# One more accumulating transfer per half block of layer 3, and wider spacing of the projection and feature pieces, in a fused four-layer attention kernel

## The chip, the cores and the metric

The kernel runs on one core of one Trainium2 chip. The metric is the device time of one execution in microseconds (us); smaller is better. Names of engines: PE is the matrix engine (PEld its weight loads), DVE the vector engine, ACT the scalar engine, POOL the GpSimd engine, SP the engine that only issues transfers (DMAs). L1698 is line 1698 of the kernel before.

## The reference, cut to what matters

The input x has four images of 64 x 64 positions with 64 channels, in float32. Four layers follow one another:

```python
# layer 0: attention over positions (n = 4096 per image)
q, k, v = x@Wq + bq, x@Wk + bk, x@Wv + bv
attn = softmax(q @ k.T)                      # 4096 x 4096 per image
x = gamma * einsum('bmn,bmc->bnc', attn, v) + x
# layer 1: layer norm, pointwise, 3x3 depthwise, gating, pointwise; twice a residual
# layer 2: attention of the rows of the image with themselves, no weights
xf = x.reshape(B, 64, 4096)                  # N = 64*64 columns per "channel"
x = einsum('bcj,bij->bci', xf, softmax(einsum('bci,bcj->bij', xf, xf))) + x
# layer 3: attention with 32 inner channels, then a normalization over all images
f = softmax(theta_x @ phi_x.T)               # 4096 x 4096 per image
w_y = (f @ g_x) @ w_W + w_b
x = x + gamma * (w_y - mean) * rsqrt(var + 0.001) + beta
```

The softmax of layer 3 needs, for every query, the sum of 4096 exponentials. How those sums are formed is what the first part of the change touches.

## The kernel before, in words

The work is one long list of items, run by `run()`: each item issues one score (or four) and what belongs to it; a schedule written by hand says which other pieces go between. The order on PE, ACT, DVE and POOL is exactly the order in which the program issues; each of these engines works its own list from the front. The stages, by the trace: layer 0 of images 0 to 3 (0 to 1026 us, with layer 1 of the earlier images laid between), layer 2 of image 0 (to 1230), layer 2 of image 1 (to 1453), layer 3 of image 0 (to 1597), layer 2 of image 2 (to 1786), layer 3 of image 1 (to 1929), layer 2 of image 3 (to 2119), layer 3 of images 2 and 3 (to 2410), and the end (to 2443). So a layer 3 block is followed by a layer 2 block, save that image 2's is followed by image 3's.

**Two lanes** carry the pieces that go between the items. A `Lane` has a clock; `misc.tick(1.8)` moves it by 1.8 at each score of layer 0 and at each item of image 0's layer 2. A piece runs when the clock has reached the lane's `next`; then `next` grows by what the piece yields. So a yield of 3.4 against ticks of 1.8 puts the pieces after ticks 1, 2, 4 and 6 of a lane that starts empty.

**The projection** `project0(b)` (L1031 on) makes q and v of image b while layer 0 of image b - 1 runs. For b > 0 it has four pieces, in the order once, v, once, v. A "once" piece has 8 matmul passes (L1037), an ACT copy out of PSUM (L1049) and a DVE copy (L1047); a "v" piece has 16 passes (L1064) and two DVE adds (L1066). Layer 0 has only two score slots in PSUM (`take_slots(0, 1)`), used in turn by scores and pieces alike: a piece takes the slot that the score after next would use.

**The features** `features2(b)` (L1303 on) transpose an image for layer 2, in four pieces: four transposes (L1310), one DVE copy and one ACT copy (L1313), two DMAs issued by SP (L1314). For image 0 they run in the lane during layer 0 of image 3, for image 1 during layer 2 of image 0 from its item 89 on (three slots there), for images 2 and 3 at fixed items of a layer 3 block, where the yielded number is not used.

**Layer 3** `layer3(b)` (from L1621) has 64 items per image: two halves (`nb`) of 32 key tiles (`mc` = 0 to 31). An item's `scores` makes 128 x 2048 scores on PE (L1646) and their exponentials e on ACT (L1657, in two or three instructions). Two items later its `products` multiplies e with the values (L1707). The e tiles come from a ring of six (`ep`, `bufs=6`), so item n + 6 writes the tile of item n. For the softmax sums, 23 of the tiles of a half are added on DVE, one after the other, into `esum` (L1696 and L1698; the first add takes tiles 0 and 1). The tiles whose `mc` is in `BY_DMA` (eight of 32) are summed instead by transfers that add to their destination: POOL issues two for each, one per half of the columns, into the tile `st["dma"]` (L1677 the first pair, which only copies, L1679 the others). One more DVE add (L1700) puts that tile into `esum`, after the products of item `by_dma[-1] + 4`. The tile comes from the pool `xn` of one buffer, which layer 2 of images 2 and 3 uses for `xr`, loaded by SP (L1368). Four items after the last tile of a half, `totals` lets PE sum `esum` over the partitions (L1719); the division and the output projection follow (L1742, L1727 to L1737, L1756). The first half of image 2 uses another list, `MORE_BY_DMA`. In the second half of image 3 tiles 30 and 31 are summed by PE (L1691), not by DVE.

Of the kernel before, what the change touches and what calls it, by code (L numbers as in the profile page):

```python
# [691 lines left out]
def fast_path(ctx: ExitStack, tc: tile.TileContext, a: dict, out: bass.AP, bad):  # L692
# [33 lines left out]
    def new_ps():  # L726
        if turn_of["banks"]:
            if turn_of["bank"] % turn_of["banks"] == turn_of["banks"] - 1:
                turn_of["bank"] += 1
            k = new_bank(), new_bank()  # L730
            return PS[:, 512 * k[0] : 512 * k[0] + 1024]
        s = turn_of["slots"][turn_of["ps"] % len(turn_of["slots"])]
        turn_of["ps"] += 1
        return PS[:, bass.ts(s, 1024)]

    def piece():
        if turn_of["banks"]:
            return PS[:, bass.ts(new_bank(), 512)]
        return new_ps()[:, 0:512]
# [8 lines left out]
    def new_e(name="e"):  # L748
        return ep.tile([128, 2048], F32, tag="e", name=name)
# [4 lines left out]
    def new_big(name):  # L754
        return big.tile([128, 4096], F32, tag="big", name=name)
# [228 lines left out]
    def tok(x, s, j):  # L984
        return x[64 * s : 64 * s + 64, bass.ts(j, 512)]
# [6 lines left out]
    def at(i, fn):  # L992
        due.setdefault(i, []).append(fn)
# [33 lines left out]
    def project0(b):  # L1027
        x, m = X[:, b], im[b]
        m.q = new_big("q")
        m.v = new_big("v")[:, 0:2048].rearrange("p (t c) -> p t c", c=C)  # L1030
        once = ((0, "once"), (0, "v"), (1, "once"), (1, "v"))  # L1031
        for j, w in once if b else ((0, "q"), (0, "v"), (1, "q"), (2, "q"), (1, "v"), (3, "q")):
            ps = new_ps()
            if w == "once":
                for o in range(2):
                    for s in range(2):
                        mm(  # L1037
                            ps[64 * o : 64 * o + 64, bass.ts(s, 512)], wq[64 * s : 64 * s + 64, 0:64],
                            tok(x, s, 2 * j + o), start=True, stop=True,
                        )  # L1040
                qs = m.q.rearrange("p (s n) -> p s n", s=2)
                for o in range(2):
                    own, other = slice(64 * o, 64 * o + 64), slice(64 - 64 * o, 128 - 64 * o)
                    n = bass.ts(2 * j + o, 512)
                    src = ps[own, :].rearrange("p (s n) -> p s n", s=2)
                    if o:
                        nc.vector.tensor_scalar_add(qs[own, :, n], src, bqk[own, :])  # L1047
                    else:
                        act(qs[own, :, n], src, AF.Identity, bias=bqk[own, :])  # L1049
                    nc.sync.dma_start(out=qs[other, :, n], in_=qs[own, :, n])  # L1050
            elif w == "q":
                for o in range(0, 128, 64):
                    for s in range(2):
                        mm(
                            ps[o : o + 64, bass.ts(s, 512)], wq[64 * s : 64 * s + 64, o : o + 64],
                            tok(x, s, j), start=True, stop=True,
                        )
                for s in range(2):
                    nc.vector.tensor_scalar_add(
                        m.q[:, 2048 * s + 512 * j : 2048 * s + 512 * j + 512], ps[:, bass.ts(s, 512)], bqk  # L1060
                    )
            else:
                for i in range(8):
                    mm(ps[:, bass.ts(i, 128)], x[:, bass.ts(8 * j + i, 128)], wv, start=True, stop=True)  # L1064
                for s in range(2):
                    nc.vector.tensor_add(  # L1066
                        m.v[:, 16 * s + 8 * j : 16 * s + 8 * j + 8, :],
                        ps.rearrange("p (t s c) -> p t s c", s=2, c=C)[:, :, s, :],
                        bv.unsqueeze(1).to_broadcast([128, 8, C]),
                    )  # L1070
            yield 3.4

# [228 lines left out]
    def features2(b):  # L1303
        x = X[:, b]
        im[b].ko = ko = new_big("ko")
        kv = ko[:, 0:N].rearrange("p (a e n) -> p a e n", e=2, n=128)
        for g in range(4):
            ps = piece()
            for i in range(4):
                nc.tensor.transpose(ps[:, bass.ts(i, 128)], x[:, bass.ts(4 * g + i, 128)], ident)  # L1310
            for e, copy in enumerate((nc.vector.tensor_copy, nc.scalar.copy)):
                own, other = slice(64 * e, 64 * e + 64), slice(64 - 64 * e, 128 - 64 * e)
                copy(kv[own, bass.ts(g, 4), e, :], ps[own, :].rearrange("p (a n) -> p a n", n=128))  # L1313
                nc.sync.dma_start(out=kv[other, bass.ts(g, 4), e, :], in_=kv[own, bass.ts(g, 4), e, :])  # L1314
            yield 3.0

    SIDES = [[(7, (h + 1) % 7), ((h + 2) % 7, (h + 3) % 7)] for h in range(7)]
    FULL = [(7, [7])] + [(h, [h] + SIDES[h]) for h in range(6)] + [(6, SIDES[6] + [6])]
# [217 lines left out]
    def close2(b):  # L1536
        x, m = X[:, b], im[b]
        ps, tot, n = piece(), sums2[:, b, :], 4 * max(m.mirrored) + 4
        cs = m.cs.rearrange("p (j k) -> p j k", k=4)
        for k in range(4):  # L1540
            mm(ps[32 * k : 32 * k + 32, 0:n], sel4, cs[:, 0:n, k], start=True, stop=True)
        g = 0
        while g < 8:
            k = g
            while k < 8 and m.count[k] == m.count[g]:
                k += 1
            nc.vector.tensor_reduce(
                tot[:, 4 * g : 4 * k],
                m.zs[:, m.first[g] : m.first[g] + 4 * m.count[g] * (k - g)]
                .rearrange("p (t k) -> p t k", k=m.count[g]), AX.X, ALU.add,  # L1550
            )
            g = k
        nc.vector.tensor_add(tot[:, 0:n], ps[:, 0:n], tot[:, 0:n])
        rz = sm.tile([128, 32], F32, tag="rz2", name="rz2")
        nc.vector.reciprocal(rz, tot)
        yield
        for i in range(4):
            ps = new_ps()
            for j in range(8):
                c = 1024 * i + 128 * j  # L1560
                nc.tensor.transpose(ps[:, bass.ts(j, 128)], m.A[:, c : c + 128], ident)
            blocks_ = ps.rearrange("p (j n) -> p j n", n=128)
            nc.vector.tensor_mul(
                blocks_, blocks_, rz[:, bass.ts(i, 8)].unsqueeze(2).to_broadcast([128, 8, 128])
            )
            xs = x[:, bass.ts(i, 512)].rearrange("p (j h) -> p j h", h=H)
            for o in range(2):
                nc.vector.tensor_add(xs, ps.rearrange("p (j o h) -> p j o h", j=8, o=2)[:, :, o, :], xs)
            yield
# [1 line left out]


    wys, early = {}, []
    BY_DMA = (2, 5, 8, 11, 14, 17, 20, 23)
    MORE_BY_DMA = (2, 4, 7, 9, 12, 14, 17, 19, 22, 24)
    small, between3 = {}, {}
    held = []
# [40 lines left out]
    def keys3(b):  # L1618
        m = im[b]
        m.ph = new_big("ph")  # L1620
        keys = m.ph.rearrange("p (s n) -> p s n", s=2)  # L1621
        for j in range(4):
            for k in range(4):
                nc.sync.dma_start(
                    out=keys[32 * k : 32 * k + 32, :, bass.ts(j, 512)],
                    in_=m.own[32 * j : 32 * j + 32, :, :],
                )

    def layer3(b):
# [3 lines left out]
        def scores(n):  # L1633
            nb, mc = n // 32, n % 32
            by_dma = MORE_BY_DMA if b == B - 2 and nb == 0 else BY_DMA
            e = es[n] = new_e()
# [46 lines left out]
        def products(n):  # L1683
            nb, mc = n // 32, n % 32
            by_dma = MORE_BY_DMA if b == B - 2 and nb == 0 else BY_DMA
            e, esum = es[n], m.tg[:, 2048:4096]
# [126 lines left out]
    conv_from, misc_from, misc_to = {}, {}, {}  # L1813
# [9 lines left out]
    for b in range(B):  # L1823
        misc_to[len(items)] = True
        f = len(items)
        if b == 0:
            layer2(b)
            misc_from[f + 89] = [features2(b + 1)]
        else:
            layer2(b, lambda b=b: keys3(b - 1))  # L1830
            turns = close2(b - 1)
            for i in (9 if b == 1 else 8, 11, 21, 31, 41):
                at(f + i, lambda turns=turns: next(turns))
            misc_from[f + 46] = [open3(b - 1)]
            f = len(items)
            misc_to[f] = True
            layer3(b - 1)
            if b + 1 < B:
                turns = features2(b + 1)
                for i in (4, 7, 10, 13):  # L1840
                    between3[f + i] = 2, lambda turns=turns: next(turns)
    f = len(items)
# [220 lines left out]
```

## Time and profile before

| what | value |
|---|---|
| median of three runs | 2442.99 us (2442.64 to 2450.58) |
| the profiled execution: its own time | 2444.88 us |
| its span in the trace | 2443.1 us |
| granted TensorE clock | 0.999 |
| busy: PE, ACT, DVE, POOL | 99%, 67%, 60%, 22% |
| layer 3 blocks together (four) | 578 us of the span (144, 143, 145, 146) |
| DVE and ACT busy in one of them (1453 to 1597) | 118.44 and 133.46 of 144 us |
| DMA engines busy in the same stage | 0.63 |

How to read it: the time is measured by the device around the whole execution, the span from the first to the last record of the trace; 1.8 us lie outside the span. Engine times are sums of instruction durations. Those of PE are modelled at their ends, and its instructions overlap, so that PE at 99% can still be waiting; what PE loses shows in the distance from one group of matmuls to the next.

### The profile page before, as it was taken

How to read it: one execution, taken by the hardware profiler on the slowest of the kernel's cores; microseconds unless marked ns; L12 is line 12 of the kernel's file. 1: busy time of each engine (PE TensorE's matmuls, PEld its weight loads, DVE VectorE, ACT ScalarE, POOL GpSimd, SP SyncE). 2: the span in 40 equal slices, each digit the busy share in tenths (PEclk: the TensorE clock that was granted, in tenths of full speed). 3: DMA queues.
4: the chain of work that ended last, by engine and by line, in shares of the span. 5: the costliest groups of instructions: out<-in, count | busy, mean ns of one | idle time of the engine just before them, and what ended most of it. 6: DMA issues, size and time to landing. Idle time of an engine off the chain costs nothing.

```text
span 2443.1 us, 63650 instructions
## 1 busy us (share of the span) xinstructions
PE 2410.9 (99%) x27509; PEld 914.5 (37%) x27509; DVE 1477.5 (60%) x1794; ACT 1642.9 (67%) x3140; POOL 541.1 (22%) x381
## 2 busy tenths in 40 slices
PE   9999999999999999999999999999999999999998
PEld 3343453336333543343344442144421344421113
DVE  2020278227732774278657668876668866688886
ACT  4656766666666666668655459954479744569996
POOL 2000000000000000030136561256631365622110
PEclk9999999999999999999999999999999999999999
DMA  3000000000000000030540027610075300386554
GB/s 80 1 18 1 19 1 18 18 19 1 19 18 5 15 19 18 21 76 2 118 92 19 20 64 138 139 28 23 16 152 118 79 22 21 76 169 141 118 116 117
DMA packets 66373, 131.68 MB, mean 54 GB/s; under 512 B 12860, under 2 KB 34085, under 8 KB 66085
## 3 DMA queue, kind: packets, MB, share of 16 engines
q0 software_dynamic: 23024, 81.83, 16.6%
q1 hardware_dynamic: 42309, 43.85, 7.9%
q8 instruction: 218, 3.57, 0.6%
q10 hardware_dynamic: 752, 1.85, 0.2%
q14 instruction: 70, 0.57, 0.1%
HBM read 4.80 MB, written 4.19 MB: 4 GB/s over the span
## 4 chain that ended last, share of the span: by engine, by line
PE 87%; DVE 5%; ACT 4%; DMA 1%; issue 1%; SPq 1%; POOL 0%; ACTq 0%; DVEq 0%; POOLq 0%
PE PS L1096 18%; PE PS L1122 18%; PE PS L1391 10%; PE PS L1453 10%; PE PS L1646 8%; PE PS L1707 8%; PE PS L1479 7%; PE PS L1206 2%; DVE tg L1698 2%; ACT e L1657 2%; DMA xn<-e 1%; ACT e L1396 1%; PE PS L1064 1%; PE PS L1171 1%; PE PS L1270 1%
## 5 line engine op out<-in xcount | busy, mean ns | idle before, releaser
L1101 ACT ACTIVATE e<-PS 128x1024 f32<-128x1024 f32 x512 | 523.7, 1023 | 339.8 <-PE PS L1096 306.5
L1396 ACT ACTIVATE e<-PS 128x512 f32<-128x512 f32 x632 | 370.9, 595 | 330.2 <-PE PS L1391 312.5
L1096 PE MATMUL PS<-X,q 64*64 64x512 f32 x4096 | 574.0, 591 | 2.3 <-DVE X L979 1.7
L1122 PE MATMUL PS<-e,vq 64*64 64x512 f32 x4096 | 575.3, 592 | 0.0
L1657 ACT ACTIVATE e<-PS 128x512 f32<-128x512 f32 (+2 forms) x588 | 500.1, 920 | 60.3 <-PE PS L1646 38.0
L1698 DVE TENSOR_TENSOR tg<-tg,e 128x2048 f32<-128x2048 f32 x172 | 393.9, 2290 | 42.7 <-ACT e L1657 31.3
L1391 PE MATMUL PS<-ko 64*64 64x512 f32 x2528 | 335.6, 596 | 1.7 <-ACT ko L1313 0.8
L1453 PE MATMUL PS<-e,X 64*64 64x512 f32 x2528 | 329.6, 590 | 1.1 <-ACT own L1465 1.1
L1432 POOL TENSOR_TENSOR esum<-esum,e 128x1024 f32<-128x1024 f32 x132 | 314.1, 2380 | 60.0 <-ACT e L1396 52.7
L1241 DVE SCALAR_TENSOR_TENSOR y<-pad,vec,y 128x1024 f32<-128x1024 f32 x240 | 308.9, 1287 | 18.2 <-ACT y L1237 10.9
L1432 POOL TENSOR_TENSOR esum<-e 128x1024 f32<-128x1024 f32 x22 | 52.2, 2373 | 1192.5 <-ACT e L1396 1184.7
L1409 DVE STREAM_TRANSPOSE turned<-e 128x1024 f32<-128x1024 f32 x196 | 240.6, 1238 | 107.5 <-ACT e L1396 107.2
L1646 PE MATMUL PS<-tg,ph 32*64 32x512 f32 x4096 | 295.7, 612 | 2.5 <-ACT e L1657 1.6
L1096 PEld LDWEIGHTS PS<-X,q 64*64 64x64 f32 x4096 | 183.0, 133 | 261.6 <-issue 181.5
L1122 PEld LDWEIGHTS PS<-e,vq 64*64 64x64 f32 x4096 | 183.1, 133 | 253.7 <-issue 158.5
L1707 PE MATMUL PS<-e,tg 128*32 128x512 f32 x2048 | 272.5, 604 | 0.0
L1109 DVE TENSOR_REDUCE sums<-zs 128x1 f32<-128x4 f32 x128 | 19.7, 154 | 276.0 <-ACT e L1101 275.9
L1679 POOL DMA_DIRECT2D xn<-e x116 | 101.0, 892 | 293.9 <-ACT e L1657 203.1
L1453 PEld LDWEIGHTS PS<-e,X 64*64 64x64 f32 x2528 | 98.0, 133 | 174.7 <-issue 155.1
L1391 PEld LDWEIGHTS PS<-ko 64*64 64x64 f32 x2528 | 90.3, 132 | 169.1 <-issue 145.1
L1646 PEld LDWEIGHTS PS<-tg,ph 32*64 32x64 f32 x4096 | 63.3, 129 | 224.4 <-ACT e L1657 192.0
L1396 ACT ACTIVATION_READ_ACCUMULATOR e<-PS 128x1 f32 x632 | 127.1, 201 | 0.0
(219 smaller groups left out, 1682.2 us busy)
## 6 DMA issues: line engine op xcount, KB each, us to landing
xn<-e POOLq DMA_DIRECT2D x132, 512.0 KB, 5.2
esum<-e POOLq DMA_DIRECT2D x20, 512.0 KB, 5.8
xn<-t SPq DMA_DIRECT2D x64, 128.0 KB
ph<-tg SPq DMA_DIRECT2D x64, 128.0 KB
xn<-X SPq DMA_DIRECT2D x224, 32.0 KB
xr<-X SPq DMA_DIRECT2D x176, 32.0 KB
ko<-ko SPq DMA_DIRECT2D x32, 128.0 KB
xr<-in_x_dram SPq DMA_DIRECT2D x13, 256.0 KB
```

The lines of the kernel that those rows point to most:

```text
L1096: mm(ps[64 * c : 64 * c + 64, bass.ts(r, 512)], m.q[rows_, 128 * t + 64 * c : 128 * t + 64 * c + 64], x[rows_, bass.ts(g, 512)], start=Tru ...
L1101: act(es[g // 2][:, bass.ts(g % 2, 1024)], ps, AF.Exp, bias=SHIFT0, accum_out=zs[:, g : g + 1],)
L1122: ins = mm(PS[64 * s : 64 * s + 64, 2048 + 512 * j : 2560 + 512 * j], vq[rows_, :], es[j // 2][rows_, k : k + 512], start=t == 0 and i < 2 ...
L1241: stt(y1, win, wt, y1, ALU.mult, ALU.add)
L1391: mm(ps[64 * c : 64 * c + 64, bass.ts(r, 512)], m.ko[rows_, k : k + 64], m.ko[rows_, bass.ts(h, 512)], start=True, stop=True,)
L1396: act(e[:, bass.ts(r, 512)], ps[:, bass.ts(r, 512)], AF.Exp, bias=SHIFT2, accum_out=slot(g, 2 * u + r),)
L1432: nc.gpsimd.tensor_add(esum, st["e"][mine_t[h][0]] if k == 1 else esum, e)
L1453: mm(st["acc"][r][64 * c : 64 * c + 64, :], xw[rows_, 4 * g + 2 * u + c, :], st["e"][n][rows_, bass.ts(c, 512)], start=n == mine[h][0], st ...
L1646: mm(PS[64 * c : 64 * c + 64, bass.ts(banks[k], 512)], m.ph[32 * k : 32 * k + 32, 128 * mc + 64 * c : 128 * mc + 64 * c + 64], m.th[32 * k ...
L1657: act(e[:, 512 * lo : 512 * k], PS[:, 512 * banks[lo] : 512 * banks[lo] + 512 * (k - lo)], AF.Exp,)
L1698: nc.vector.tensor_add(esum, esum, e)
L1707: mm(st["y"][32 * k : 32 * k + 32, :], m.gx[:, i % 32, :], es[i][:, bass.ts(k, 512)], start=mc == 0, stop=i % 32 == 31,)
```

## The change

```diff
@@ project0
-            yield 3.4
+            yield 3.7 if b else 3.4
@@ features2
-            yield 3.0
+            yield 3.7
@@ layer 3
-    BY_DMA = (2, 5, 8, 11, 14, 17, 20, 23)
+    BY_DMA = (2, 5, 8, 11, 14, 17, 20, 23, 26)
     MORE_BY_DMA = (2, 4, 7, 9, 12, 14, 17, 19, 22, 24)
@@ the schedule, at layer 2 of image 0
         if b == 0:
             layer2(b)
-            misc_from[f + 89] = [features2(b + 1)]
+            misc_from[f + 88] = [features2(b + 1)]
```

In seven of the eight half blocks of layer 3, tile 26 is summed by two more accumulating transfers in place of a DVE add, and the add of the transfers' tile into `esum` moves from after the products of item 27 to after those of item 30. The first half of image 2 keeps its list. The projection's pieces for images 1 to 3 and the features' pieces in the lane yield 3.7. Features of image 1 start one item earlier. Nothing else changes: the same matmuls, exponentials and copies are issued.

## The prediction, made before the changed kernel was run

> **What bounds the kernel now.** I read the page first, then the waits, then the timeline around each place that the diff touches. The page says that PE is always busy, and that ACT and DVE are not:
>
> ```profile
> PE 2410.9 (99%) x27509; PEld 914.5 (37%) x27509; DVE 1477.5 (60%) x1794; ACT 1642.9 (67%) x3140; POOL 541.1 (22%) x381
> L1698 DVE TENSOR_TENSOR tg<-tg,e 128x2048 f32<-128x2048 f32 x172 | 393.9, 2290 | 42.7 <-ACT e L1657 31.3
> ```
>
> The 99% is soft. Inside layer 0 a score group (8 passes) starts 1.72 us after the one before it, product included; that is PE's own pace. In layer 3 an item has 16 score passes, eight side by side, and 8 product passes, four side by side: again four rounds, 1.72 us at layer 0's 0.43 a round. Yet items start 2.04 us apart, which is ACT's pace (1.94 us of exponentials and a gap of about 0.1). So a microsecond taken from DVE counts only where something waits for DVE. The group of the sums over partitions names that place:
>
> ```profile
> L1719 PE MATMUL PS<-tg,ones 128*32 128x512 f32 x64 | 8.5, 601 | 2.6 <-DVE tg L1698 2.6
> ```
>
> PE idles 2.6 us in all before these sums because DVE has not finished adding. The first such place, at the middle of image 0's block (DVE first, then PE and ACT):
>
> ```profile
> 1508.00 9.48 DVE L1698 TENSOR_TENSOR tg<-tg,e 128x2048 f32<-128x2048 f32 x4 [1.37 <-ACT e L1657]
> 1517.52 2.29 DVE L1700 TENSOR_TENSOR tg<-tg,xn 128x2048 f32<-128x2048 f32 x1
> 1519.91 9.48 DVE L1698 TENSOR_TENSOR tg<-tg,e 128x2048 f32<-128x2048 f32 x4
> ...
> 1527.42 1.57 PE L1646 MATMUL PS<-tg,ph 32*64 32x512 f32 x16
> 1529.54 1.06 PE L1719 MATMUL PS<-tg,ones 128*32 128x512 f32 x8 [0.55 <-DVE tg L1698]
> 1532.53 1.95 ACT L1657 ACTIVATE e<-PS 128x512 f32<-128x512 f32 x2 [1.44 <-PE PS L1646]
> ```
>
> DVE adds tiles 24 to 27, the transfers' tile, then 28 to 31: nine adds, one every 2.39 us, without a gap; items come every 2.04 us, so the backlog grows to the end. PE stands 0.55 us, and ACT then 1.44 us. The other three places show 0.55 (1862.36), 0.61 (2277.21) and this:
>
> ```profile
> 2345.86 1.06 PE L1719 MATMUL PS<-tg,ones 128*32 128x512 f32 x8 [0.84 <-DVE tg L1698]
> ```
>
> At the blocks' ends before a layer 2 (1599.36 and its twin) and in the tail (2409.95) PE is itself late, and no such idle is shown.
>
> For the spacing, compare image 1's projection, where "once" and "v" are already two scores apart, with image 2's, where the first two pieces are one score apart:
>
> ```profile
> 154.68 1.04 PE L1096 MATMUL PS<-X,q 64*64 64x512 f32 x8
> 155.54 1.04 PE L1122 MATMUL PS<-e,vq 64*64 64x512 f32 x8
> 156.70 1.09 PE L1096 MATMUL PS<-X,q 64*64 64x512 f32 x8
> 157.72 2.05 PE L1064 MATMUL PS<-wv,X 128*128 128x128 f32 x16
> ```
>
> ```profile
> 375.62 1.30 PE L1096 MATMUL PS<-X,q 64*64 64x512 f32 x8
> 376.54 1.29 DVE L1047 TENSOR_SCALAR q<-PS,bqk 64x1024 f32<-64x1024 f32 x1 [2.36 <-ACT q L1049]
> 377.89 2.05 PE L1064 MATMUL PS<-wv,X 128*128 128x128 f32 x16 [0.97 <-DVE q L1047]
> ```
>
> The "v" piece takes the slot that "once" used, and DVE empties that at 377.83 only. Two scores later it would have been free.
>
> **What the Trainium skill says.** "Perfetto Trace Analysis", section "Tensor Engine Instruction (MATMUL, LD_WEIGHTS)": PE's end times are computed, not observed, while ACT and DVE are strict queues. The trace agrees: PE at 99% has starts 0.3 us late, as above, and I therefore price by starts. "SBUF — State Buffer", section "SBUF: two separate sides": compute and DMA can't slow each other there, and a DVE operation with two SBUF inputs loses only to a GpSimd operation that reads SBUF. The trace agrees: the adds take 2.29 us whether transfers run or not. "DMA: Bandwidth & Descriptors", section "Issuing engines are not separate DMA queues": all transfers share 16 engines. In the trace a pair of accumulates fills them: busy share 1.0 at about 200 GB/s for about 5.3 us of every 6.1 (three items).
>
> **The change, part by part.**
>
> Layer 3, DVE. In seven half blocks one add of 2.39 us goes. The tail of a half becomes 24, 25, 27, 28, 29, 30, transfers' tile, 31. Image 0: exp(24) ends at 1507.96 and exp(27) three items later, at 1514.1; DVE has finished 25 at 1512.7 and waits 1.4 us. From 1514.1 six adds of 2.39 end at 1528.4, against 1529.40 now. So 2.39 - 1.4 = 1.0 us is gained on DVE, and the sums could start at 1528.5; but the scores before them end at 1528.99 by the record. PE is next late, and the gain is the idle shown, 0.55 us. Same working: image 1 61.2 against 62.2, gain 0.55; end of image 2, 76.1 against 77.1, gain 0.61; middle of image 3, 44.3 against 45.7, gain 0.84. Sum 2.55 us. From below, 0, if PE's record hides another wait; from above, the whole excess of the distance over 2.04 + 0.86 (an item and the sums): 3.97 - 2.90 = 1.07 three times and 1.51 once, 4.7 us. I take 2.55: ACT idles 1.4 to 1.8 us behind each place, so that PE's gain is passed on.
>
> The other three halves gain nothing. At the ends of images 0 and 1 DVE finishes at 1597.0 in place of 1597.97, and PE reaches the sums at 1599.36 either way. In the tail PE is in L1691 until 2410.1 and DVE has ended at 2409.56; then 2408.6.
>
> Layer 3, transfers: two more of 512 KB per half, each 0.87 us of POOL's issue. POOL has nothing after them until the next half's first pair (1529.50) or layer 2's sums (1604.67), so the issue costs 0. The pair of tile 23 leaves the DMA engines at 1512.9, 1846.5, 2261.0 and 2329.0 in the middle halves, and 2398.2 in the tail; another 5.3 us brings tile 26 to 1518.2, 1851.8, 2266.3, 2334.3 and 2403.5. Two things wait for it. Tile 32's exponential reuses the e tile, at 1522.35, 1855.2, 2269.95, 2338.3: cover 3.4 to 4.2 us. The add of the transfers' tile, now about 2406.3 in the tail: cover 2.8 us. Behind the waiting DVE add stands only tile 31's add, then PE's sums. Cost 0 while the cover holds.
>
> The moved add frees `xn` later: at 1525.9 for 1519.8 in the middle, where the next half's first transfer starts at 1529.50 (cover 3.6), and at 1594.6 for 1588.4 before layer 2, where SP's loads wait for it. The 16 loads of `xr` land at 1598.1 now, 1604.3 then; PE needs them at 1612.69 (L1479). Cover 8.4 us, cost 0; the next 16 loads follow on SP's queue for a use some 25 us later.
>
> Projection. Image 2: from the score at 375.62 to that at 394.56 are seven intervals of 1.72, a "once" of 0.86 and two "v" of 1.98, which is 16.86; it took 18.94, so 2.08 is lost. Image 1, already spaced, from 152.10 to 174.26: 21.16 of work, 22.16 taken, 1.0 lost. The lane's sums put the pieces after ticks 1, 3, 5, 7 instead of 1, 2, 4, 6; image 2 becomes like image 1: 1.0 us gained, and image 3 (18.95 for the same stretch) likewise. Image 1's own second piece goes from two to three scores after the first: 0. Together 2.0, between 1.0 (if the conv work on DVE makes the copy late) and 2.4.
>
> Features of image 0: each piece costs 0.17 us in a stretch of 18.46, none waits for another; spacing changes nothing. Features of image 1: pieces after items 88, 90, 92, 94 instead of 89, 90, 92, 94. The second piece now comes one item after the first, and the score behind it waits:
>
> ```profile
> 1219.90 1.09 PE L1391 MATMUL PS<-ko 64*64 64x512 f32 x8 [0.82 <-ACT ko L1313]
> ```
>
> One item earlier the first ACT copy ends at about 1217.7 instead of 1219.85; exp(89) then stands behind it (1219.2 for 1217.5) but exp(90) ends at 1220.6 for 1221.2, and the second piece's copy at 1223.15 for 1223.6. Gain 0.45, between 0 and 0.8. Its DMAs on SP shift with it, ahead of nothing.
>
> **Sum**: 2.55 + 2.0 + 0.45 = 5.0 us off the profiled execution, 2444.88 to 2439.9, with the span from 2443.1 to 2438.1. That execution stood 1.9 us over the median of the runs shown; off the median, 2442.99 - 5.0 = **2438.0 us**, or 0.2% less. About 0.3% (7.3 us) is what a measurement of this kernel can tell from no change, so the likeliest case counts as no change.
>
> **Rivals.**
> *More than the idle shows.* PE's modelled ends hide part of the wait: 4.7 in layer 3, 2.4 + 0.8 elsewhere, and up to 0.8 for what follows the sums: 8.7 us, 2434.3. For it: ACT's idle exceeds PE's. Against: the score group at 1527.42 is stretched to 1.57 by held exponentials, not by DVE.
> *Only the spacing shows.* Layer 3 runs at ACT's pace and takes the DVE time back: 2.45 us off, 2440.5. Against it stand the four named idles.
> *Slower: the ninth pair holds its tile.* If tile 26 lands more than about 9 us after tile 23's pair (5.3 reckoned), exp(32) waits, and from 8.1 us the tail's add. The longest landing of one such transfer is 9.7 us. At 12 us the four middles lose 2.5 + 3.3 + 3.1 + 2.7, the tail 2.4 (3.9 late, less the 1.5 by which DVE would lead PE), 14.0 in all, and 2.45 of the gain is left: 11.5 slower, 2454.5. Against: spacing stays at three items, as for the eight before, and nothing else moves then.
>
> **Chances.** Forecast 0.58, more 0.22, only spacing 0.12, slower 0.08. Forecast and spacing lie within 0.3%: 0.70; the larger gain lies beyond it: 0.22; the slower case 0.08. Range: from 2433.5 (just under all upper bounds) to 2444.0 (all gains zero, and 1 us for moved pieces), leaving out the slower case and a little on both sides.
>
> **What would show it.** 172 adds at L1698 become 165 and L1679 has 130 issues for 116. The idle before L1719 falls from 2.6 us to near 0, and DVE waits about 1.4 us before tile 27. The stretches of images 2 and 3 take about 17.9 us. Wrong would be: an exponential or L1700 waiting for a transfer, L1479 waiting for `xr`, or layer 3's middles unchanged with the idle before L1719 gone.

## The result and the profile after

The changed kernel takes **2439.2 us** (2438.12 to 2440.64, 16 runs) beside 2445.05 (2442.48 to 2450.58, 16 runs) for the kernel before on the same chips: a ratio of 0.9975, with a 95% interval of 0.9968 to 0.9982. By that ratio it is 6.1 us less (4.4 to 7.8), by the medians 5.9. The executions of the kernel before reach further up (a quarter of them above 2446.9 us) than those of the changed kernel, and the lower quartiles, 2442.90 and 2438.75, are only 4.2 us apart. The forecast was 2438.0 us, as 5.0 us less than 2442.99. Its base turned out low: over more runs the kernel before has a median of 2444 to 2445.6.

The profiled execution of the changed kernel has its own time of 2438.81 us, a span of 2437.0 and a granted clock of 0.999. The engines and three groups, from the page and the list of groups (columns as before: busy us and mean ns, then the idle time ahead and what ended it):

```profile
PE 2408.3 (99%) x27509; PEld 914.1 (38%) x27509; DVE 1461.6 (60%) x1787; ACT 1643.0 (67%) x3140; POOL 553.5 (23%) x395
L1698 DVE TENSOR_TENSOR tg<-tg,e 128x2048 f32<-128x2048 f32 x165 | 377.8, 2290 | 51.1 <-ACT e L1657 40.9
L1679 POOL DMA_DIRECT2D xn<-e x130 | 113.3, 898 | 319.5 <-ACT e L1657 225.9
L1719 PE MATMUL PS<-tg,ones 128*32 128x512 f32 x64 | 8.5, 602 | 2.2 <-DVE tg L1698 1.1 <-ACT e L1657 1.1
```

165 adds and 130 issues: the change does what it says. But the idle ahead of the sums over partitions (L1719) is 2.2 us, not near 0. Of it 1.1 stand in one place, the middle of image 2's block, whose list the change leaves alone; there it comes and goes (none when the changed kernel ran again). The other 1.1 are new: four times 0.26, in the four places of the forecast, and ended by **ACT**. The timeline of the changed kernel at the middle of image 0's block (start, busy us, engine and line; lines of other work left out):

```profile
1509.91 9.49 DVE L1698 TENSOR_TENSOR tg<-tg,e 128x2048 f32<-128x2048 f32 x4 [1.43 <-ACT e L1657]
1519.43 2.29 DVE L1700 TENSOR_TENSOR tg<-tg,xn 128x2048 f32<-128x2048 f32 x1
...
1521.22 0.58 ACT L1713 COPY yz<-PS 128x512 f32<-128x512 f32 x1 [0.44 <-PE PS L1707]
1521.70 5.19 ACT L1657 ACTIVATE e<-PS 128x1536 f32<-128x1536 f32 x6
1521.83 2.29 DVE L1698 TENSOR_TENSOR tg<-tg,e 128x2048 f32<-128x2048 f32 x1
...
1523.21 1.57 PE L1646 MATMUL PS<-tg,ph 32*64 32x512 f32 x16
...
1525.04 1.06 PE L1719 MATMUL PS<-tg,ones 128*32 128x512 f32 x8 [0.26 <-ACT e L1657]
...
1528.04 1.94 ACT L1657 ACTIVATE e<-PS 128x512 f32<-128x512 f32 x2 [1.15 <-PE PS L1646]
```

DVE waits 1.43 us ahead of tile 27 and then runs tiles 27 to 30, the transfers' tile and tile 31 without a gap, as forecast. It ends at 1524.12, 0.9 us before the sums start. ACT is what is late now: it copies the finished products (L1713), then runs exponentials without a pause.

**Where the time went, by a ladder.** Both kernels run the same 1732 exponentials in the same order. I took the start of each in one trace less its start in the other; where that lag steps and stays, time is won.

| place | forecast | ladder |
|---|---|---|
| first loads (second exponential) | 0 | 0.68 |
| projection, images 1, 2, 3 | 0, 1.0, 1.0 | 0, 0.77, 0.79 |
| features of image 1 | 0.45 | 1.11 |
| layer 2 of image 0, 1237 to 1247 us | 0 | 0.86 |
| layer 3 middles and end: 1529, 1862, 2277, 2346 us | 0.55, 0.55, 0.61, 0.84 | 0.29, 0.29, 0.35, 0.58 |
| middle of image 2, unchanged list | 0 | 0.37 |
| sum | 5.0 | 6.1 |

So three rows of the forecast are there, each with another size, and three rows are not in it. The experiments had to say which rows belong to the change. The first score groups of image 2's projection and of image 1's features in the changed kernel, for the two spacings:

```profile
374.94 1.30 PE L1096 MATMUL PS<-X,q 64*64 64x512 f32 x8
375.80 1.30 PE L1122 MATMUL PS<-e,vq 64*64 64x512 f32 x8
377.21 1.09 PE L1096 MATMUL PS<-X,q 64*64 64x512 f32 x8
378.23 2.05 PE L1064 MATMUL PS<-wv,X 128*128 128x128 f32 x16
```

```profile
1214.76 0.58 ACT L1313 COPY ko<-PS 64x512 f32<-64x512 f32 x1 [0.77 <-DVE ko L1313]
...
1215.39 0.65 PE L1310 MATMUL PS<-ident,X 128*128 128x128 f32 x4 [0.17 <-ACT ko L1313]
...
1216.89 1.04 PE L1391 MATMUL PS<-ko 64*64 64x512 f32 x8
...
1219.66 0.58 ACT L1313 COPY ko<-PS 64x512 f32<-64x512 f32 x1 [1.88 <-DVE ko L1313]
```

The "v" piece (L1064) no longer waits 0.97 us for the copy on DVE, and the score at L1391 no longer waits 0.82 us for the copy on ACT.

### The profile page after: what moved, and what is told of

Read it like the earlier page. It is cut to its first block, busy times and chain, and to the rows that moved or that the text cites. A ratio compares the mean times of both kernels' runs of the same rounds, so it can differ in the third digit from the quotient of the medians.

```text
span 2437.0 us, 63657 instructions
## 1 busy us (share of the span) xinstructions
PE 2408.3 (99%) x27509; PEld 914.1 (38%) x27509; DVE 1461.6 (60%) x1787; ACT 1643.0 (67%) x3140; POOL 553.5 (23%) x395
## 4 chain that ended last, share of the span: by engine, by line
PE 90%; DVE 4%; ACT 4%; issue 1%; DMA 0%; SPq 0%; ACTq 0%; DVEq 0%
PE PS L1096 18%; PE PS L1122 18%; PE PS L1391 10%; PE PS L1453 10%; PE PS L1646 9%; PE PS L1707 9%; PE PS L1479 7%; PE PS L1206 2%; ACT e L1657 2%; DVE tg L1698 1%; ACT e L1396 1%; PE PS L1171 1%; PE PS L1270 1%; PE PS L1561 1%; PE PS L1064 1%
## 5 line engine op out<-in xcount | busy, mean ns | idle before, releaser
L1698 DVE TENSOR_TENSOR tg<-tg,e 128x2048 f32<-128x2048 f32 x165 | 377.8, 2290 | 51.1 <-ACT e L1657 40.9
L1391 PE MATMUL PS<-ko 64*64 64x512 f32 x2528 | 334.3, 596 | 0.9 <-DVE X L1568 0.5
L1679 POOL DMA_DIRECT2D xn<-e x130 | 113.3, 898 | 319.5 <-ACT e L1657 225.9
L1391 PEld LDWEIGHTS PS<-ko 64*64 64x64 f32 x2528 | 90.0, 132 | 167.8 <-issue 145.5
```

The costliest lines, as they stand in the source:

```text
L1391: mm(ps[64 * c : 64 * c + 64, bass.ts(r, 512)], m.ko[rows_, k : k + 64], m.ko[rows_, bass.ts(h, 512)], start=True, stop=True,)
L1698: nc.vector.tensor_add(esum, esum, e)
```

## The experiments

In each run the kernel before ran on the same chip. The us are the ratio's interval on a time before of 2444.

| kernel | median us | before | ratio (95%) | us against before |
|---|---|---|---|---|
| spacing only | 2441.03 | 2444.3 | 0.9984 (0.9976 to 0.9991) | -5.9 to -2.2 |
| projection only | 2442.43 | 2445.15 | 0.9991 (0.9984 to 0.9998) | -3.9 to -0.5 |
| features only | 2442.91 | 2444.1 | 0.9993 (0.9987 to 1.0000) | -3.2 to 0 |
| ninth tile only | 2441.96 | 2444.3 | 0.9989 (0.9983 to 0.9996) | -4.2 to -1.0 |
| changed, again | 2438.84 | 2444.3 | 0.9975 (0.9967 to 0.9983) | -8.1 to -4.2 |
| before, again | 2445.61 | 2444.3 | 1.0007 (0.9999 to 1.0015) | -0.2 to 3.7 |
| tile 26 left out | 2442.58 | 2444.1 | 0.9994 (0.9988 to 1.0001) | -2.9 to 0.2 |
| changed, cut after two | 2439.44 | 2444.1 | 0.9979 (0.9970 to 0.9989) | -7.3 to -2.7 |
| changed, tile 28 left out | 2439.47 | 2444.1 | 0.9976 (0.9967 to 0.9985) | -8.1 to -3.7 |
| changed, copy on DVE | 2453.28 | 2445.15 | 1.0033 (1.0021 to 1.0045) | 5.1 to 11.0 |
| before, copy on DVE | 2466.35 | 2445.15 | 1.0086 (1.0073 to 1.0099) | 17.8 to 24.2 |
| changed, 28 left out, copy first | 2436.20 | 2444.17 | 0.9964 (0.9950 to 0.9978) | -12.2 to -5.4 |

My theory after seeing the traces: the spacing is worth 2.7 us, the ninth tile 1.5, since ACT takes DVE's place as the last at the sums; the rest is what differs between executions. The rivals: the ladder is drift; DVE still sets the places; the transfers cost something.

### The spacing and the ninth tile apart

```diff
-            yield 3.4
+            yield 3.7 if b else 3.4
-            yield 3.0
+            yield 3.7
-            misc_from[f + 89] = [features2(b + 1)]
+            misc_from[f + 88] = [features2(b + 1)]
```

> The kernel before with the wider spacing alone (projection, features and their earlier start), eight transferred tiles as before. Theory now: 1.6 us from the projections of images 2 and 3, 1.2 from the features of image 1, and 0 to 0.9 from two slips of half a round on PE behind them (L1453 and L1391, 1237 to 1242), so 2.8 to 3.6 us less than before. The forecast's own sum for this part: 2.45. Rival that the ladder between the two traces is only drift from one execution to the next: within 0.5 us of before. Rival that all of the change's gain is the spacing: 5.8 us less.

```diff
-    BY_DMA = (2, 5, 8, 11, 14, 17, 20, 23)
+    BY_DMA = (2, 5, 8, 11, 14, 17, 20, 23, 26)
```

> The kernel before with the ninth transferred tile alone, spacing as before. Theory now: of the idle of 0.55, 0.55, 0.61 and 0.84 before the sums over partitions, 0.26 stays in each place because the sums' PSUM bank is released last by the exponential of item 34, so 0.3 + 0.3 + 0.35 + 0.58, or 1.5 us less than before; each of the four sums shows 0.26 idle behind ACT and none behind DVE. The forecast: 2.55 less. Rival that more was hidden than the idle: 4.7 less. Rival that the transfers cost something: less than 1 us gained, with an exponential or L1700 waiting for a DMA.

Measured, by medians: 3.3 us less for the spacing, 2.3 for the ninth tile. The two add up to 5.6, and the whole change gives 5.5 in the same series (5.9 in the first measurement). Neither half alone makes the result, so the rival that all of it is spacing falls (its 5.8 is at the edge of the interval, and the ninth tile's interval excludes 0). The ninth tile's interval takes in both 1.5 and the forecast's 2.55 and excludes 4.7; the ladder tells the first two apart. In the trace of the ninth tile alone the steps in the four places are 0.30, 0.29, 0.35 and 0.58, and each sum has 0.26 idle behind ACT, none behind DVE.

### Projection and features apart

Each with its own lines of the diff above.

> The kernel before with the projection's spacing alone (3.7 in place of 3.4 for images 1 to 3). Theory now: 0.78 us in each of images 2 and 3 and nothing in image 1, 1.6 less than before; the score behind the first piece still waits about 0.55 us for the slot that DVE empties. The forecast's own term: 2.0. Rival that this part is worth nothing: within 0.3 us.

> The kernel before with the features' pieces alone changed: 3.7 in place of 3.0 and a start one item earlier. Theory: 1.2 us less than before, and up to 2.0 if the two slips of half a round behind them go too. The forecast's own term: 0.45. Rival that the features' part is worth nothing: within 0.3 us.

Measured: 2.7 and 1.2 us less by medians. In the trace of the projection alone the lag steps by 0.78 at image 2 and 0.78 at image 3 and not at image 1; in that of the features alone by 1.1 at image 1's features, and at image 0's features it moves and comes back to 0. So both theory sizes hold in the traces to a tenth; the intervals of the times are too wide to tell 1.6 from 2.0, or 1.2 from 0.45.

### What differs between executions

Both kernels unaltered.

> The kernel before once more, unaltered, for what differs between executions. Theory: the ratio is 1; idle of about 0.55, 0.55, 0.61 and 0.84 behind DVE at the four sums; the first exponential within 0.6 us of either trace at hand, since the first loads vary; the two slips of half a round behind the features of image 1 are there again if they belong to the kernel, and absent if they are chance.

> The changed kernel once more, unaltered, for what differs between executions. Theory: the same 0.26 idle in four places, the same starts of the features' pieces and no slip of half a round behind the features of image 1 in its trace; about 5.8 us less than before. If the slips come and go from one execution to the next, they belong to neither kernel.

The kernel before, again, has a span of 2441.2 us, 1.9 below the first trace of the same kernel: 1.18 at the second exponential and 0.86 at 1237 to 1247, of which 0.1 is lost again by the end of the span. The same score of layer 2 in the first trace of before:

```profile
1237.25 1.47 PE L1453 MATMUL PS<-e,X 64*64 64x512 f32 x7
...
1238.11 1.03 PE L1391 MATMUL PS<-ko 64*64 64x512 f32 x3
...
1238.55 0.59 PE L1453 MATMUL PS<-e,X 64*64 64x512 f32 x1
1238.56 1.01 PE L1391 MATMUL PS<-ko 64*64 64x512 f32 x4
```

and in the second trace of before:

```profile
1236.10 1.04 PE L1453 MATMUL PS<-e,X 64*64 64x512 f32 x8
...
1236.96 1.04 PE L1391 MATMUL PS<-ko 64*64 64x512 f32 x8
```

In the first a matmul of one group runs late and the groups interleave; in the second each has its eight. From the 706th exponential to the 716th it takes 15.07 to 15.14 us in ten of the fourteen traces, and 15.57 (before with the copy on DVE), 15.93 (the first trace of before), 16.18 (tile 26 left out) and 16.37 (tile 28 left out) in the others. These slips belong to neither kernel. The second exponential starts between 14.22 and 15.56 us, also without regard to the kernel. And from the 1501st exponential to the 1531st, around the middle of image 2, the two traces of before take 32.45 and 32.38, those of the changed kernel 31.98 and 32.33: the latter differ by 0.35 between themselves, and the spacing alone has 31.62, so by these traces the row of 0.37 can't be called the change's. My expectation that the slips would tell the kernels apart fell.

What the ladder leaves to the change is 1.56 + 1.11 + 1.51 = 4.2 us. The interval of the measured gain begins at 4.4, but the lower quartiles of the two kernels are 4.2 us apart (4.8 in the experiments), and the traces account for most of that. The rest of the 6.1 goes with executions that the kernel before has and the changed one lacks. In the experiments 45 of 152 executions of the kernel before took over 2446 us, and none of the 30 of the changed kernel, its first measurement included, took over 2442.14. Of the 24 above 2448 us, 17 have a granted clock of 0.997, where all 30 of the changed kernel have 0.998 or 0.999. None of that length was profiled, so what lengthens them, and whether the change ends it, stays open.

### Do the transfers cost anything?

Tile 26 is neither added on DVE nor transferred; the sums of the softmax lack it in seven halves.

```diff
-            elif mc and mc not in by_dma:
+            elif mc and mc not in by_dma and (mc != 26 or by_dma is MORE_BY_DMA):
```

> The kernel before with the DVE add of tile 26 left out in the same seven halves, and no transfer in its place: tile 26 is missing from the sums of the softmax. The add of the transfers' tile stays after the products of item 27. Theory: DVE gains what it gains in the change, and the transfers cost nothing, so the same as the ninth tile alone, about 1.5 us less than before (1.0 to 2.0). Rival that the transfers take something back: 1 us or more beyond the ninth tile alone. Rival that DVE is what bounds these places all the way: 2.39 us a place, over 4 us less.

Measured: 1.5 us less than before by medians (between 2.9 less and 0.2 more), where the ninth tile with its transfers gives 2.3 (4.2 to 1.0). The four steps against the second trace of before are 0.28, 0.31, 0.35 and 0.58, those of the ninth tile alone to a few hundredths. The transfers cost nothing that can be seen (the intervals overlap, and the steps agree), and DVE doesn't bound these places all the way, or each would have given up to 2.39.

### Is DVE still last?

The changed kernel with tile 28 left out of the sums too, in the same seven halves.

```diff
-            elif mc and mc not in by_dma:
+            elif mc and mc not in by_dma and (mc != 28 or by_dma is MORE_BY_DMA):
```

> The changed kernel with the DVE add of tile 28 left out as well in the seven halves: tile 28 is missing from the sums of the softmax. DVE is then another 2.4 us earlier at the four places. Theory: DVE has already ceased to be last there, so no further gain, within 0.4 us of the changed kernel, with 0.26 idle behind ACT at the sums as before. Rival that DVE still sets the places: 1 us or more below the changed kernel.

Measured: 2439.47 us, no gain over the changed kernel's 2438.84 to 2439.2. The timeline of this kernel at the same middle:

```profile
1521.99 2.29 DVE L1698 TENSOR_TENSOR tg<-tg,e 128x2048 f32<-128x2048 f32 x1
...
1524.04 1.57 PE L1646 MATMUL PS<-tg,ph 32*64 32x512 f32 x16
...
1525.87 1.07 PE L1719 MATMUL PS<-tg,ones 128*32 128x512 f32 x8 [0.26 <-ACT e L1657]
```

DVE ends at 1524.28, 1.6 us before the sums and so another 0.7 ahead (not 2.4 as I expected: it waits for exponentials in between, 1.84 us ahead of tile 29). The sums start 1.83 us after the scores at 1524.04, and 1.83 after those at 1523.21 in the changed kernel. DVE has ceased to matter there; the rival falls.

### Is it the bank that the exponentials hold?

The third exponential of each following half is issued in two instructions, cut after one bank of four; here after two.

```diff
-            cut = between3[first + n][0] if first + n in between3 else 1
+            cut = between3[first + n][0] if first + n in between3 else 2 if mc == 2 and (nb or last) else 1
```

> The changed kernel, with the exponential of item 34 (the third of each following half) cut after two banks in place of one, so that its second part, which holds the bank that the sums use, is shorter and earlier lines up differently. Theory: if the bank is what leaves 0.26 idle in each of the four places, the sums start when PE is ready, and up to 1.0 us goes: 1.0 to 6.8 us less than before in all, that is 0.5 to 1.0 below the changed kernel; the idle behind ACT at the sums is gone or altered by the shift of the exponentials' ends. Rival that the idle of 0.26 is only a gap that the record's modelled ends make: no change. Rival that the longer first part holds PE's scores back: slower than the changed kernel by up to 1 us.

Measured: 2439.44 us, no better than the changed kernel. The timeline at the same middle:

```profile
1523.79 2.00 PE L1646 MATMUL PS<-tg,ph 32*64 32x512 f32 x16
...
1525.71 1.07 PE L1719 MATMUL PS<-tg,ones 128*32 128x512 f32 x8
```

The 0.26 behind ACT is gone, but the scores ahead stretch from 1.57 to 2.00, and the sums start 1.92 us after them instead of 1.83. So the 0.26 was a real wait for an exponential, and where it is cut only decides whether the scores or the sums wait. The lag's steps are 0.1 us smaller in each of the four places than in the changed kernel: of the expected 1.0 us nothing came, and the rival that the longer first part holds the scores back happened in small.

### Taking the copy off ACT

ACT's work there is the copy of the finished products (L1713) and then six exponentials. First I moved the copy to DVE, behind the add of tile 31 (lines from there on stand one further down).

```diff
-                nc.scalar.copy(st["yz"][:, 0:512], st["y"])
+                copy = nc.vector.tensor_copy if nb == 0 or b == 2 else nc.scalar.copy
+                copy(st["yz"][:, 0:512], st["y"])
```

> The changed kernel with one more edit: where a half is followed by more of layer 3, the copy of the products out of PSUM (L1713, 0.58 us on ACT, with 0.44 of idle ahead of it) goes to DVE, behind the add of tile 31. Theory: after the change ACT is what comes last at the four middles, since its exponentials of items 33 and 34 queue behind that copy; without it the scores of item 34 are no longer stretched from 1.11 to 1.57 and the 0.26 ahead of the sums goes, so 0.7 us a place at four or five places, 2.5 to 3.6 us below the changed kernel, until DVE's last add (1524.12 in the first middle) is the bound again. Rival that the exponentials take the room and nothing is gained: within 0.5 us of the changed kernel. Rival that the copy's 0.69 us on DVE makes the next half's products wait: slower.

> The kernel before, with eight transferred tiles and the old spacing, and the same copy (L1713) on DVE at the same places. Theory: DVE's last add comes last there (1529.40 in the first middle), so taking work off ACT only turns PE's stretched scores into idle behind DVE: within 0.5 us of before, with the idle behind DVE at the sums up from 2.6 to about 4.5 us. Rival that ACT bounds these places whatever DVE does: as much as in the changed kernel, 2.5 to 3.6 us less than before.

Both became much slower: 14.4 us over the changed kernel (2453.28 - 2438.84) and 21.2 over before. My theory's numbers failed for both, and the third rival named for the changed kernel (the next half's products wait) happened, at a price I had not worked out. The changed kernel with the copy on DVE:

```profile
1521.34 2.29 DVE L1698 TENSOR_TENSOR tg<-tg,e 128x2048 f32<-128x2048 f32 x1
1523.55 0.68 DVE L1714 COPY yz<-PS 128x512 f32<-128x512 f32 x1
...
1524.28 1.07 PE L1707 MATMUL PS<-e,tg 128*32 128x512 f32 x8 [2.57 <-DVE yz L1714]
1525.28 1.11 PE L1646 MATMUL PS<-tg,ph 32*64 32x512 f32 x16
1526.32 1.07 PE L1720 MATMUL PS<-tg,ones 128*32 128x512 f32 x8
```

The products of all items sum into one bank. Item 32's, which begin the next half, stand on PE ahead of the scores of item 34, and wait until the copy has emptied the bank: 2.57 us here, 13.5 in five places. With eight tiles the same wait is 3.65, 3.64, 3.97 and 3.70 us in four of them, 18.9 in all. So the order on DVE (copy behind the last add) turned DVE's lateness into PE's.

The waits are not the whole price. Behind some of them PE itself runs slower, as at the end of image 2 in the changed kernel with the copy on DVE:

```profile
2276.82 1.94 PE L1707 MATMUL PS<-e,tg 128*32 128x512 f32 x8 [2.57 <-DVE yz L1714]
2278.69 1.86 PE L1646 MATMUL PS<-tg,ph 32*64 32x512 f32 x16
```

In the timeline above the same groups take 1.07 and 1.11. The granted clock of the trace is 0.51 from 2276.8 to 2280.3, and 1.00 around the wait at 1524. It is about half behind two of the five waits here, for 3.4 us each, and with eight tiles behind all five, for 3.4 or 6.8 us, 23.9 in all. The three places without the drop lose 1.8 to 2.1 us against the first trace of the changed kernel, the two with it 3.4 and 3.3. A wait of 3.20 us was not followed by the drop and two of 2.57 were, so its length alone doesn't decide.

The pair also shows what the same ninth tile is worth where DVE is what PE waits for. With the copy on DVE, the changed kernel is 13.1 us faster than before (2466.35 - 2453.28); less 3.3 for the spacing that is about 10 us, where with the copy on ACT it is 1.5 to 2.3. In the two traces 5.4 us of it are shorter waits (18.9 - 13.5); the time at half clock falls too, from 23.9 to 6.8 us. How the 10 us divide between the two wasn't separated.

Last, the copy ahead of the add, with DVE given time: the kernel with tile 28 left out of the sums (lines from there on stand two to six further down).

```diff
+            elif mc == 31 and (nb == 0 or b == 2):
+                pass
...
-                nc.scalar.copy(st["yz"][:, 0:512], st["y"])
+                if nb == 0 or b == 2:
+                    nc.vector.tensor_copy(st["yz"][:, 0:512], st["y"])
+                    nc.vector.tensor_add(esum, esum, e)
+                else:
+                    nc.scalar.copy(st["yz"][:, 0:512], st["y"])
```

> The changed kernel with tile 28 left out of the sums of the softmax, as in the dose run, and the copy of the products (L1713) on DVE at the five places where more of layer 3 follows, now ahead of the add of tile 31, so that neither the copy nor the add comes late. Theory: the exponentials behind that copy on ACT are what comes last after the change, so with the copy gone from ACT, and DVE in time, the scores of item 34 take 1.11 again and the 0.26 goes: 0.7 to 0.8 us at each of five places, 3 to 4 us below the changed kernel. Rival that PE's own order of work is what is left there and ACT isn't: within 0.5 us of the changed kernel. Rival that the products of item 32 still wait for the copy, 0.1 to 0.4 us a place: a gain of 1 to 2 us only.

Measured: 2436.20 us, 3.3 below the kernel with tile 28 left out (2439.47) and 2.6 to 3.0 below the changed kernel. The intervals of the ratios overlap, but the slowest of its five executions (2436.71) is below the quickest of either of the others. Its timeline:

```profile
1521.53 0.69 DVE L1716 COPY yz<-PS 128x512 f32<-128x512 f32 x1 [0.17 <-PE PS L1709]
1522.14 2.28 DVE L1717 TENSOR_TENSOR tg<-tg,e 128x2048 f32<-128x2048 f32 x1
1522.43 1.07 PE L1709 MATMUL PS<-e,tg 128*32 128x512 f32 x8
...
1523.43 1.11 PE L1646 MATMUL PS<-tg,ph 32*64 32x512 f32 x16
1524.58 1.07 PE L1725 MATMUL PS<-tg,ones 128*32 128x512 f32 x8
```

The scores are back at 1.11 us, the 0.26 is gone, and the sums start 1.15 us after the scores instead of 1.83. The lag against the run with tile 28 left out steps by 0.6 to 0.8 in the four places; the fifth, in the middle of image 2, gains nothing, and its products waited 1.56 us for the copy. So the total stays a little under the 3 to 4 us expected below the changed kernel. ACT's queue of copy and exponentials was what stood next behind DVE: the two kernels differ only in that copy, and in the add of tile 31 that now follows it. This kernel lacks a tile in its sums, so it is no version to use. With tile 28 kept, DVE would reach tile 31 some 0.7 us later (the difference measured above) and by my estimate eat most of this; it wasn't tried.

## Why the prediction was right, and where not

**Right in sign and nearly in size.** The total, 5.0 us, lies within the measured 4.4 to 7.8, though the traces show only 4.2 of it, in other sizes than forecast. "More than the idle shows" (8.7 us less) and "only the spacing shows" (2.45) lie outside it. "Slower: the ninth pair holds its tile" did not happen. That a difference under 7.3 us can't be told from no change did not hold for sixteen executions of each kernel: the interval excludes 0.

**Layer 3, DVE: one term of the sum failed.** DVE's own times came as worked out: the wait of 1.4 us before tile 27, no gap after it, about 1 us won. But "PE is next late, and the gain is the idle shown" was wrong. ACT is next late, and 0.26 of each idle stays: 0.55, 0.55, 0.61 and 0.84 became 0.29, 0.29, 0.35 and 0.58, or 1.51 for 2.55, the difference being 4 x 0.26 to the hundredth. That ACT stood there is shown twice: more time on DVE bought nothing, and taking the copy off ACT did. The trace of before held the hint. ACT idled 1.44 us after the place, and I read that as room; but its exponentials just ahead of it stretched the scores from 1.11 to 1.57, and it was those that the sums met next. I had named that stretch, but only as an argument against the larger rival.

**Layer 3, transfers at 0: right.** No exponential of a half with the new list waits for a transfer. The only wait of the kind is 0.50 us in image 2's first half, 2.2 in the first trace of before, where the list is the same. A transfer takes 5.3 us to land at the median, 5.2 before. L1700 runs without a gap before it in the timeline above. The matmuls that read `xr` in layer 2 of images 2 and 3 (L1479, listed under the pool's name `xn`) idle 0.5 us in all, and that is put down to DVE. Leaving out add 26 without a transfer gives no more than the change.

**Ends of images 0 and 1 and the tail at 0: right.** The ladder has no step there.

**Projection: right in kind, 1.56 for 2.0.** Image 1 gains nothing, images 2 and 3 gain 0.77 and 0.79 for 1.0 each. Image 2's stretch takes 18.17 us (374.94 to 393.11), not 17.9. The term that was too small is the wait that spacing leaves: the score behind the "once" piece takes its slot, and comes at 377.21 instead of 376.66, 0.55 late (DVE empties the slot at 377.15), where image 1 loses 0.30 at that point. I carried image 1's loss of 1.0 over to image 2; it is 1.3.

**Features of image 0 at 0: right. Features of image 1: 1.11 for 0.45.** The step that failed is the length of ACT's queue. I let the second copy end at 1223.15; shifted by the lag there (2.24), it ends at 1222.48, 0.67 earlier. The two exponentials of a score take 1.16 us there (1215.36 to 1216.52), and I had reckoned 1.4 to 1.5 in line behind the first copy.

**The base.** The median of three runs, 2442.99, was 1 to 2.6 us below the medians of larger samples. So that 2438.0 comes so near 2439.2 is partly luck. Its parts miss by more (layer 3 and projection 1.5 us over, features 0.7 under), its base is low, and the measured gain holds about 1.9 us that no part of it names.

## What to carry to other kernels

When the engine that comes last at a wait is relieved, look up where **each other** engine stands at that instant, those with idle time behind the place too: the gain ends at the second latest, and a stretched group just ahead of the wait names it. Before moving an instruction to an idler engine, follow what its result releases and what stands behind that waiter in its queue: 0.6 us in each of five places, moved from ACT to DVE, cost 14 us in waits and slower matmuls. And with effects of 1 us in 2440, take two traces of the same kernel before a difference between two is called the change's.

## What the hardware showed beyond expectation

- The same ten exponentials of layer 2, which no kernel here alters, took 15.07 to 16.37 us, and 15.93 and 15.07 in two executions of the kernel before, with matmuls of neighbouring groups falling out of step by about 0.43 us. What starts it isn't shown.
- Behind ten waits of PE of 2.57 to 3.99 us (the copy on DVE, nine and eight tiles) the granted clock stood at about half in seven cases, for 3.4 or 6.8 us. What decides between the cases isn't shown.
- Seven pairs more of accumulating transfers left the landing time of one as it was (5.3 us, from 5.2), though a pair fills the DMA engines (busy share 1.0 in the prediction's windows of the trace before).
- The first loads shift the whole execution by up to 1.3 us (second exponential at 14.22 to 15.56 us).
